# A transformer block in one kernel: the gated layer's second projection in seven products for three of its four blocks, its last bias spread over half units, four copies on ScalarE

## The chip, the core and the metric

The kernel runs on one core of one Trainium2 chip. The metric is the device time of one execution in microseconds, as the median of several executions. All arithmetic is in 32-bit floats.

## What is computed

Two batch rows of 1024 tokens with 256 features go through self-attention (16 heads of 64), cross-attention to 154 context rows, and a gated feed-forward layer, each with a layer norm ahead of it and a residual behind it. What matters here is the last layer:

```python
h = _layernorm(x, ln3_g, ln3_b)
p = h @ ff_w1 + ff_b1                      # 256 -> 2 x 1024
a, gate = (p[..., :D_FF], p[..., D_FF:])
h = a * jax.nn.gelu(gate, approximate=False) @ ff_w2 + ff_b2   # 1024 -> 256
return h + x
```

## The kernel before

The program is laid out by hand: the order in which it is written is the order in which each engine gets its instructions, and semaphores are added where one engine's result or buffer is needed by another. Three stages follow each other: self-attention, cross-attention, and the gated layer, a loop over `k` from 0 to 63. All of the change but one switch lies in that last loop; the switch is in a function that both of the last two stages call.

**Blocks, units, half units.** The 2048 tokens are four blocks ("pairs", `pair` 0 to 3) of 512 tokens, each again two halves of 256 (`BT`). The 1024 inner features are eight groups of 128 (`NF`). A unit `n` is one block and one group, `k` counts half units: even `k` runs `gate_first(k // 2)`, odd `k` runs `gate_second(k // 2)`. The first projection (`product`, L1039) already takes seven products for eight: for a unit TensorE runs products 1, 6 and 5 in the first half unit, 2, 7 and 3 in the second, and 4 (`gate_last`) in the next unit's first half, after that unit's product 1. Product 4 goes onto product 7's PSUM tile `pb` and so waits for VectorE's read of it (L1078). Each product is one call of 128x128 weights against 256 columns. ScalarE copies the first sum (L1058) and does the two Gelus (L1076, L1082); VectorE adds (L1062, L1064, L1078, L1081, L1090); GpSimd multiplies value and gate into `ub[pair]` (L1083 for the second half of the block's tokens, L1092 for the first).

**The second projection** (`sum_slot`, L1105). When the last group of a block is done, 32 slots are put in the list `sums`: four row tiles of 128 tokens, eight inner groups each, one call of 256 columns per slot. Two slots are taken in each half unit, so block 0's run in half units 16 to 31, block 1's in 32 to 47, block 2's in 48 to 63, and block 3's after the loop. After the eighth slot of a row tile VectorE adds the sum to the rows in `xt` (L1115) and a DMA sends them out, on SP's queue, or on ScalarE's for every second tile of the last block.

**Work beside it.** `side` is a list of steps of layer norms: from half unit 7 on the second batch row's norm runs, one step in each odd half unit (statistics on VectorE; deviation and normalized rows `xn` on GpSimd, L246, L250, L267; four transposes on TensorE into `ph`, L280; scaling on ScalarE). `later` is a list of small steps, one of which is taken in each half unit; in this loop they are the 16 additions of the last bias to the rows of `xt` on GpSimd (L320), eight for each batch row, put there when that row's norm is through. `token_sums` puts four GpSimd additions in half units 8, 24 and 40, for the first projection of the next block.

**Cross-attention's last two units** are finished inside the loop: `cross_values` multiplies into four PSUM tiles `poc` and copies each with VectorE (L930); part 0 uses two tiles of one PSUM pool, part 1 two of the pool `mm` from which the products' tiles `pa` come as well.

Of the kernel before, what the change touches and what calls it, by code (L numbers as in the profile page):

```python
# [18 lines left out]
def tile_transformer_block(ctx: ExitStack, tc: tile.TileContext, a: dict, out: bass.AP):  # L19
    nc = tc.nc  # L20
    x, cond = a["x"], a["ctx_768"]
# [10 lines left out]
    NT = S // P  # L32
    GT = 4
    NG = NT // GT
# [5 lines left out]
    KB = 32  # L40
# [22 lines left out]
    pt_ = ctx.enter_context(tc.tile_pool(name="pt", bufs=2))  # L63
# [33 lines left out]
    row_of, r = {}, 0  # L97
    for n in names:
        k = n_of[n]
# [458 lines left out]
    later = []  # L558
# [11 lines left out]
    def run_work(n, n_side, bank=None, n_sum=0):  # L570

        while n > 0 and work:
            n -= work[0].banks
            run(work.pop(0))
        for _ in range(min(n_side, len(side))):
            needs_bank, needs, fn = side[0]
            if needs_bank and not bank and n <= 0 or not added.issuperset(needs):  # L580
                break
            if needs_bank and not bank:
                n -= 1
            spare["bank"] = bank or mm_tile
# [316 lines left out]
    def cross_values(ui, a2):  # L901

        b, pr = units[ui]
        v, v0 = vs["ca", b, pr // 2], pr % 2 * P
        if a2 == 0 and pr % HP == 0:
            oT["ca", b, pr // HP] = pt_.tile([P, HP, S], F32, tag="oT", name=f"o_ca{b}_{pr}")
        quarters = (a2, 2 + a2)  # L910
        po = {a4: (mm_tile if a2 else sum_tile)(f"poc_{ui}_{a4}") for a4 in quarters}
        for m in range(NM + 1):
            for a4 in quarters:
                r0 = a4 // 2 * QG
                r = slice(r0, r0 + QG)
                for j in range(2):
                    nc.tensor.matmul(  # L917
                        po[a4][j * DH:(j + 1) * DH, :NT * KB],
                        lhsT=v[r, m + a2 * (m == NM), v0 + j * DH:v0 + (j + 1) * DH],
                        rhs=pTc["pairs"][r, a2, m, j] if m < NM else  # L920
                        pTc["ring"][r, ui % 3, NB - 1, j, :],
                        start=(m == 0), stop=(m == NM),
                        tile_position=(r0, j * DH),
                    )
        dst = oT["ca", b, pr // HP][:, pr % HP, :].rearrange(
            "p (t a q) -> p t a q", a=P // KB, q=KB)

        def store():
            for a4 in quarters:
                nc.vector.tensor_copy(  # L930
                    dst[:, :, a4, :], po[a4][:, :NT * KB].rearrange("p (t q) -> p t q", q=KB)
                )

        return store

# [26 lines left out]
    NPR = B * 2  # L962
    BT = S // 4
    FU = NPR * NF
    wsum, wh, ub, psum, pools = {}, {}, {}, {}, {}

    def hold_gated():

        wf = pt_.tile([P, 2 * NK, QH // 2], F32, tag="pT", name="wf").rearrange("p a b -> p (a b)")
        n1, n2 = NC * 2 * DF, NF * D  # L970
        w1 = wf[:, :n1].rearrange("p (c h f) -> p c h f", c=NC, h=2)
        w2 = wf[:, n1:n1 + n2].rearrange("p (f d) -> p f d", f=NF)
        pTc["pairs"] = wf[:, n1 + n2:n1 + n2 + 2 * NM * 2 * NT * KB].rearrange(
            "p (a m j q) -> p a m j q", a=2, m=NM, j=2)
# [15 lines left out]
        parts.extend(lambda f=f: part2(f) for f in range(0, NF, 2))  # L990
        return w1, w2, parts
# [39 lines left out]
    def product(n, i, into, first):  # L1031

        pair, f = divmod(n, NF)
        own = slice(f * P, (f + 1) * P)
        lhs = {
            1: w1[:, 0, 1, own], 2: w1[:, 1, 1, own], 3: wsum[4][:, own], 4: w1[:, 1, 0, own],
            5: wsum[1][:, own], 6: wsum[2][:, own], 7: w1[:, 0, 0, own],
        }[i]
        nc.tensor.matmul(  # L1039
            into[:, :BT], lhsT=lhs, rhs=wh[pair][i], start=first, stop=True,  # L1040
            skip_group_check=True)
# [24 lines left out]
    def biases(n):  # L1066
        c = row_of["ff_b1"] + n % NF
        return cols[:, c:c + 1], cols[:, c + NF:c + NF + 1]
# [16 lines left out]
    def gate_last(n):  # L1085

        pair, f = divmod(n, NF)
        pa, pb, pc, own = psum.pop(n)
        product(n, 4, pb, False)
        nc.vector.scalar_tensor_tensor(  # L1090
            own[:, 0, :], pb[:, :BT], biases(n)[0], own[:, 0, :], op0=ALU.add, op1=ALU.add)
        nc.gpsimd.tensor_tensor(ub[pair][0][:, f, :], own[:, 0, :], own[:, 3, :], ALU.mult)  # L1092
        if f == NF - 1:
            sums.extend((pair, i, e) for i in range(2 * TF) for e in range(NF))

    sums, summed = [], {}

    def sum_slot():

        pair, i, f = sums.pop(0)  # L1100
        if f == 0:
            summed[pair] = sum_tile(f"pf{pair}_{i}")
        own = summed[pair]
        j, e = divmod(i, TF)
        nc.tensor.matmul(  # L1105
            own[:, :D], lhsT=ub[pair][j][:, f, e * P:(e + 1) * P], rhs=w2[:, f, :],
            start=(f == 0), stop=(f == NF - 1),
        )
        if f < NF - 1:
            return None  # L1110
        b, t = divmod(pair * 2 * TF + i, NT)

        def store():
            xs = xt[b, t // GT][:, t % GT, :]
            nc.vector.tensor_tensor(xs, own[:, :D], xs, ALU.add)  # L1115
            (nc.scalar if pair == NPR - 1 and i % 2 else nc.sync).dma_start(
                out=out[b, t * P:(t + 1) * P, :], in_=xs)

        return store


    with tc.manual_schedule():
# [11 lines left out]
        own = [ps_s.tile([P, 2, HB], F32, tag="s", name=f"first_{r}") for r in range(2)]  # L1134
# [49 lines left out]
        for p in range(SA):  # L1184
# [11 lines left out]
            ui, n = divmod(p, 2 * SH)  # L1196
# [5 lines left out]
            if p < 2 * SH - 1 or p % SH in (1, 2):  # L1202
# [4 lines left out]
                f = (ui - NPAIR // 2 - 1) * EC  # L1207
# [12 lines left out]
        for c in range(CA):  # L1220
# [7 lines left out]
            if c == SH + 1:  # L1228

                w1, w2, parts = hold_gated()  # L1230
# [3 lines left out]
            ui, n = divmod(c, len(CG))  # L1234
# [75 lines left out]
        for k in range(2 * FU):  # L1310
            c = CA + k
            if k == 0:
                run_work(0, 0, n_sum=2)
            flush(adds)
            (gate_second if k % 2 else gate_first)(k // 2)
            flush(stores)
            flush(lates)
            if k == 2 * len(CG) + 1:
                norm_beside("ff", B - 1)
            if k == 0:  # L1320
                load_out("ca", B - 1, NQ - 1)
            cross_drain(c)
            if k % 2:
                cross_weigh(c - 1 if k == len(CG) + 2 else c)
            cross_regroup(c)
            if k == len(CG) + 2:
                out_pieces("ca", B - 1, NQ - 1, out_order("ca"))
            if k % (2 * NF) == NF and k < 2 * FU - 2 * NF:
                token_sums(k // (2 * NF) + 1)
            for _ in range(min(2, len(sums))):  # L1330
                run(sum_slot)
            flush(stores)
            run_work(0 if k == 1 else 1 + k % 2, k % 2)
            if later:
                later.pop(0)()
        gate_last(FU - 1)
        while sums:
            run(sum_slot)
            flush(stores)
# [33 lines left out]
```

## Time and profile before

| | |
|---|---|
| median of 3 runs | 1095.6 us (1094.71 to 1096.67) |
| the profiled execution | 1093.61 us, span 1091.8 us |
| granted TensorE clock | 0.998 |
| TensorE matmuls, busy | 1070.7 us, 98% of the span |
| GpSimd, busy | 729.9 us, 67% |
| first call of the second projection | 960.9 us from the span's start |
| its last call | 1088.2 us |

Times in the profile count from the span's start. A 32-bit matmul call shows as two records of the matmul (PE) and two of its weight load (PEld), so "x2" after a matmul is one call. A record's length contains its way through the array, so consecutive records overlap, and the distance from one start to the next tells what a record costs. In a timeline the bracket behind a line is the time that the engine was idle before it, and what ended that. The span is a little shorter than the execution's time, which has start and end around it.

### The profile page before, as it was taken

What the parts mean: (1) busy time and instruction counts of PE and PEld (TensorE: products, weight loads), DVE (VectorE), ACT (ScalarE), POOL (GpSimd) and SP (SyncE); (2) the same over time, 40 slices, a digit from 0 to 9 for tenths busy, and PEclk for the clock granted to TensorE, in tenths of its full rate; (3) what the DMA queues carried; (4) which work ended last, traced back from release to release, by engine and by line L of the source; (5) the groups of instructions that cost most, each with busy time, mean ns of one, the idle gap of its engine ahead of it and who ended that gap; (6) DMA issues with size and microseconds to landing.
All of it is one profiled execution on the core that took longest, in us unless ns stands there. A gap on an engine that the chain in (4) does not pass through costs nothing.

```text
span 1091.8 us, 44847 instructions
## 1 busy us (share of the span) xinstructions
PE 1070.7 (98%) x18388; PEld 703.4 (64%) x18388; DVE 881.2 (81%) x1301; ACT 643.5 (59%) x2057; POOL 729.9 (67%) x1552
## 2 busy tenths in 40 slices
PE   8999999999999999999999999989999999899998
PEld 6446556556566565566565665566767677788887
DVE  5799899998988989999989989868877877645442
ACT  5666766777667666667776775566555554232221
POOL 2677777877777777777777777667664785565321
PEclk9999999999999999999999999999999999999999
DMA  3222112112111111111111211136755555000000
GB/s 94 64 60 67 43 38 52 33 33 57 40 43 39 42 44 29 42 43 34 42 42 30 46 33 29 32 85 159 187 133 127 127 117 133 1 10 15 11 15 30
DMA packets 106142, 62.81 MB, mean 58 GB/s; under 512 B 32330, under 2 KB 96722, under 8 KB 105938
## 3 DMA queue, kind: packets, MB, share of 16 engines
q1 hardware_dynamic: 104562, 59.16, 22.7%
q8 instruction: 145, 2.38, 0.9%
q10 hardware_dynamic: 1376, 0.79, 0.2%
q14 instruction: 59, 0.48, 0.1%
HBM read 30.01 MB, written 2.10 MB: 29 GB/s over the span
## 4 chain that ended last, share of the span: by engine, by line
PE 89%; DVE 3%; POOL 3%; ACT 2%; DMA 2%; SPq 1%; issue 1%; ACTq 0%; DVEq 0%; POOLq 0%
PE s L493 19%; PE po L547 19%; PE py_sa L467 5%; PE pf L1105 5%; PE py_ca L467 5%; PE pv_sa L393 5%; PE pq_sa L362 5%; PE pk_sa L362 4%; PE poc L917 4%; PE pq_ca L362 4%; PE pb L1039 3%; PE sc L838 3%; PE pa L1039 2%; PE pc L1039 2%; PE ph_ln L280 1%; ACT p L508 1%
## 5 line engine op out<-in xcount | busy, mean ns | idle before, releaser
L613 POOL TENSOR_SCALAR p<-p,rd,ee 128x512 f32<-128x512 f32 x512 | 390.3, 773 | 98.1 <-DVE rd L605 93.7
L508 ACT ACTIVATE p<-s,st 128x512 f32<-128x512 f32 x512 | 345.8, 687 | 177.9 <-DVE st L502 168.9
L502 DVE TENSOR_REDUCE st<-s 128x2 f32<-128x1024 f32 x256 | 308.8, 1207 | 53.4 <-issue 16.8
L626 DVE STREAM_TRANSPOSE pT<-p 128x1024 f32<-128x1024 f32 x256 | 302.6, 1220 | 4.0 <-POOL p L613 4.0
L493 PE MATMUL s<-k_sa,q_sa 64*32 64x512 f32 x4096 | 252.0, 594 | 4.9 <-ACT p L508 4.2
L547 PE MATMUL po<-pT,v_sa 64*32 64x256 f32 x8192 | 235.8, 376 | 2.3 <-DVE pT L626 2.3
L547 PEld LDWEIGHTS po<-pT,v_sa 64*32 64x32 f32 x8192 | 169.2, 106 | 80.6 <-issue 27.1
L493 PEld LDWEIGHTS s<-k_sa,q_sa 64*32 64x32 f32 x4096 | 79.5, 106 | 106.6 <-issue 51.2
L854 ACT ACTIVATE p<-sc,neg 128x154 f32<-128x154 f32 x256 | 96.5, 407 | 83.3 <-DVE rden L862 77.2
L865 POOL TENSOR_SCALAR p<-p,rden 128x154 f32<-128x154 f32 x256 | 97.3, 401 | 60.0 <-DVE rden L862 59.6
L508 ACT ACTIVATION_READ_ACCUMULATOR p<-s,st 128x1 f32 x512 | 103.4, 202 | 0.0
L526 POOL TENSOR_TENSOR dd<-st 128x8 f32<-128x8 f32 x128 | 25.8, 202 | 68.7 <-DMA st<-st 65.5
L393 PEld LDWEIGHTS pv_sa<-sa_wv,hT_ln 64*128 64x128 f32 x1024 | 58.6, 188 | 14.2 <-issue 10.1
L393 PE MATMUL pv_sa<-sa_wv,hT_ln 64*128 64x128 f32 x1024 | 61.8, 275 | 0.0
L467 PE MATMUL py_ca<-ca_wo,o_ca 128*128 128x256 f32 x256 | 60.0, 382 | 0.5 <-DVE o_ca L930 0.5
L467 PE MATMUL py_sa<-sa_wo,o_sa 128*128 128x256 f32 x256 | 59.7, 386 | 0.0
L467 PEld LDWEIGHTS py_sa<-sa_wo,o_sa 128*128 128x128 f32 x256 | 47.3, 190 | 17.8 <-issue 6.2
L843 DVE TENSOR_REDUCE neg<-sc 128x6 f32<-128x924 f32 (+1 forms) x48 | 48.0, 1000 | 13.2 <-PE sc L838 13.1
L362 PE MATMUL pq_ca<-hT_ln,ca_wq 64*128 64x512 f32 (+1 forms) x304 | 58.2, 589 | 0.0
L854 ACT ACTIVATION_READ_ACCUMULATOR p<-sc,neg 128x1 f32 x256 | 57.1, 223 | 0.0
L362 PE MATMUL pq_sa<-hT_ln,sa_wq 64*32 64x512 f32 (+1 forms) x976 | 56.6, 586 | 0.0
L362 PE MATMUL pk_sa<-hT_ln,sa_wk 64*32 64x512 f32 x960 | 55.5, 590 | 0.0
(117 smaller groups left out, 1418.3 us busy)
## 6 DMA issues: line engine op xcount, KB each, us to landing
wf<-pT_ca SPq DMA_DIRECT2D x128, 128.0 KB, 2.4
st<-st SPq DMA_DIRECT2D x512, 1.0 KB, 1.8
v_sa<-v_sa SPq DMA_DIRECT2D x32, 256.0 KB, 4.1
sa_wq<-in_L_xattn_sa_wq_dram SPq DMA_DIRECT2D x32, 128.0 KB, 3.0
sa_wk<-in_L_xattn_sa_wk_dram SPq DMA_DIRECT2D x32, 128.0 KB, 2.9
sa_wv<-in_L_xattn_sa_wv_dram SPq DMA_DIRECT2D x32, 128.0 KB, 3.2
ca_wq<-in_L_xattn_ca_wq_dram SPq DMA_DIRECT2D x32, 128.0 KB, 3.7
wf<-in_L_xattn_ff_w_dram SPq DMA_DIRECT2D x12, 256.0 KB, 3.3
```

What stands on the lines that cost most here:

```text
L362: nc.tensor.matmul(pq[r][f:f + m, at:at + n], lhsT=wt[own, c, f:f + m], rhs=h[own, c, t0:t0 + n], start=(c == 0), stop=(c == NH - 1), tile ...
L393: nc.tensor.matmul(pv[r][:, i * P:(i + 1) * P], lhsT=h[own, c, i * P:(i + 1) * P], rhs=wt[own, c, :], start=(c == 0), stop=(c == NH - 1), ...
L467: nc.tensor.matmul(py[:, e * D:(e + 1) * D], lhsT=o[:, i, (t + e) * P:(t + e + 1) * P], rhs=wo[kind, b, g][:, i, :], start=(i == 0), stop= ...
L493: nc.tensor.matmul(sc[a4 * KB:(a4 + 1) * KB, j, :], lhsT=q[r, c:c + KB], rhs=k[r, h * HB:(h + 1) * HB], start=True, stop=True, tile_positi ...
L502: nc.vector.tensor_reduce(st[:, 0, 0, i, :], sc, AX.X, ALU.max, negate=True)
L508: nc.scalar.activation(pr[:, j, :], sc[:, j, :], AF.Exp, bias=st[:, 0, 0, i, j:j + 1], accum_out=st[:, 0, 1, i, j:j + 1],)
L547: nc.tensor.matmul(po[a2][d:d + KB, :QH // 2], lhsT=v[r, t, e, d:d + KB], rhs=pT[r, d // DH * NK + n, :], start=(t == 0 and e == 0), stop= ...
L613: nc.gpsimd.tensor_scalar(pr[:, j, :], pr[:, j, :], v["rd"][:, c:c + 1], v["ee"][:, 0, c:c + 1], op0=ALU.mult, op1=ALU.mult,)
L626: nc.vector.transpose(halves[h][:, :, c:c + KB], slot[p]["members"][i].rearrange("p j (n k) -> p (j n) k", k=KB))
L854: nc.scalar.activation(pr_[:, j, i, :T], sc[:, j, i * T:(i + 1) * T], AF.Exp, bias=neg[:, j, i:i + 1], accum_out=den[:, j, i:i + 1],)
L865: nc.gpsimd.tensor_scalar(pr_[:, j, i, :T], pr_[:, j, i, :T], rden[:, j, i:i + 1], 1.0, op0=ALU.mult, op1=ALU.mult,)
L1039: nc.tensor.matmul(into[:, :BT], lhsT=lhs, rhs=wh[pair][i], start=first, stop=True, skip_group_check=True)
```

## The change

Four things are changed.

1. In `cross_values`, when the gated layer's PSUM pool is open, one of the two copies of each part goes to ScalarE. This holds for the two units that are finished inside the loop, four copies in all.
2. The steps in `later` are taken only when `k > 12` and `k % 3 == 1`, so the 16 bias additions fall in half units 13, 16, 19 and so on to 58.
3. For blocks 1 to 3 the second projection takes seven products for eight. The block's tokens and the inner groups (even and odd) form a two by two matrix of `ub`; the inner groups and the output's two halves of 128 columns form one of the weights. Four sums of weights (`column_sums`, 128x512 each) are made once, in half units 18, 20, 24 and 26; four sums of `ub` (`row_sums`, 128x256 each) are made for each pair of inner groups, four times a block, from half unit 21 on, all on GpSimd, the last four after the loop. They lie in the buffer that held cross-attention's transposed weights. A slot is then one product for one of two row tiles: four calls of 128x128 weights against 128 columns. There are 14 slots a block; block 0 keeps its 32 slots of before, two in a half unit, and from half unit 32 on there is one slot in a half unit. A row tile's sums go into two PSUM tiles, `into` (products 2, 3, 4, 5, in four column ranges) and `own` (product 1 in the first 128 columns, product 6 in the next, and product 7 added onto product 6 after VectorE has read that).
4. The sums of the seven products are formed by the residual additions on VectorE: after product 1 to all four quarters (128x512), after 6 to one (128x128), after 3 from `into` to all four (128x512) and from its last range once more to one (128x128), after 7 to two (128x256). Rows of the first half go out after product 3, of the second after 7. The last block's slots run in the order 1, 4, 2 for both row tiles, then 5, 6, 3, 7 for one and for the other.

```diff
+        shared = pools.get("f") is not None
         def store():
             for a4 in quarters:
-                nc.vector.tensor_copy(
-                    dst[:, :, a4, :], po[a4][:, :NT * KB].rearrange("p (t q) -> p t q", q=KB)
-                )
+                own = po[a4][:, :NT * KB].rearrange("p (t q) -> p t q", q=KB)
+                if shared and a4 == a2:
+                    nc.scalar.copy(dst[:, :, a4, :], own)
+                else:
+                    nc.vector.tensor_copy(dst[:, :, a4, :], own)
...
         if f == NF - 1:
-            sums.extend((pair, i, e) for i in range(2 * TF) for e in range(NF))
+            if pair:
+                early, late = (1, 4, 2), (5, 6, 3, 7)
+                if pair == NPR - 1:
+                    sums.extend((pair, i, m) for m in early for i in range(TF))
+                    sums.extend((pair, i, m) for i in range(TF) for m in late)
+                else:
+                    sums.extend((pair, i, m) for i in range(TF) for m in early + late)
+            else:
+                sums.extend((pair, i, e) for i in range(2 * TF) for e in range(NF))
...
+    def column_sums(n):
+        t = half["t"]
+        nc.gpsimd.tensor_tensor(*[
+            lambda: (t[5], quarter(0, 1), quarter(0, 0)),
+            lambda: (t[6], quarter(1, 1), t[5]),
+            lambda: (t[4], quarter(1, 0), t[6]),
+            lambda: (t[7], quarter(1, 1), quarter(0, 1)),
+        ][n](), ALU.subtract)
+
+    def row_sums(pair, c):
+        s = {i: own[:, c, :] for i, own in half["s"][pair % 2].items()}
+        (a11, a12), (a21, a22) = ([ub[pair][j][:, 2 * c + e, :] for e in range(2)] for j in range(2))
+        tt = nc.gpsimd.tensor_tensor
+        tt(s[5], a21, a22, ALU.add)
+        tt(s[6], s[5], a11, ALU.subtract)
+        tt(s[3], a12, s[6], ALU.subtract)
+        tt(a21, a11, a21, ALU.subtract)
+
+    def partial(pair, i, m):
+        if m == 1:
+            bank = mm_tile if pair == NPR - 1 and i else sum_tile
+            summed[pair, i] = [bank(f"pf{pair}_{i}_{r}") for r in range(2)]
+        into, own = summed[pair, i]
+        at = {2: 0, 3: 1, 4: 2, 5: 3}.get(m)
+        region = own[:, (m != 1) * P:][:, :P] if at is None else into[:, at * P:(at + 1) * P]
...
+        for c in range(NF // 2):
...
+            nc.tensor.matmul(
+                region, lhsT=lhs, rhs=rhs, start=(c == 0 and m != 7), stop=(c == NF // 2 - 1),
+                skip_group_check=True)
+        if m in (2, 4, 5):
+            return None
...
+        def store():
+            if m == 1:
+                plus(xs, region.unsqueeze(1).unsqueeze(1).broadcast_to([P, 2, 2, P]))
+            elif m == 6:
+                plus(xs[:, 0, 1], region)
+            elif m == 3:
+                plus(xs, into.rearrange("p (j d k) -> p j d k", j=2, d=2))
+                plus(xs[:, 0, 1], into[:, 3 * P:4 * P])
+                send(0, nc.sync)
+            else:
+                plus(xs[:, 1], region.unsqueeze(1).broadcast_to([P, 2, P]))
+                send(1, nc.scalar if pair == NPR - 1 and i else nc.sync)
...
-            (nc.scalar if pair == NPR - 1 and i % 2 else nc.sync).dma_start(
-                out=out[b, t * P:(t + 1) * P, :], in_=xs)
+            nc.sync.dma_start(out=out[b, t * P:(t + 1) * P, :], in_=xs)
...
-            for _ in range(min(2, len(sums))):
+            for _ in range(min(2 if k < 4 * NF else 1, len(sums))):
                 run(sum_slot)
             flush(stores)
             run_work(0 if k == 1 else 1 + k % 2, k % 2)
-            if later:
+            if later and k > 12 and k % 3 == 1:
                 later.pop(0)()
+            if k == 2 * NF:
+                hold_sums()
+            if k in (2 * NF + 2, 2 * NF + 4, 2 * NF + 8, 2 * NF + 10):
+                column_sums((k - 2 * NF) // 3)
+            pair, at = divmod(k - 5, 2 * NF)
+            if pair > 0 and at % 4 == 0:
+                row_sums(pair, at // 4)
         gate_last(FU - 1)
+        row_sums(NPR - 1, NF // 2 - 1)
         while sums:
             run(sum_slot)
             flush(stores)
```

More of the change, by code (lines that the diff above doesn't have):

```diff
@@ new lines, in tile_transformer_block, with hold_sums @@
+    sums, summed = [], {}
+    half = {}
+    def hold_sums():
+        wx = pt_.tile([P, 2 * NK, QH // 2], F32, tag="pT", name="wx").rearrange("p a b -> p (a b)")
+        n1, n2 = NF // 2 * P, NF // 2 * BT
+        half["t"] = {
+            i: wx[:, k * n1:(k + 1) * n1].rearrange("p (c d) -> p c d", d=P)
+            for k, i in enumerate((5, 6, 7, 4))
+        }
+        half["s"] = [
+            {
+                i: wx[:, 4 * n1 + (3 * e + k) * n2:][:, :n2].rearrange("p (c t) -> p c t", t=BT)
+                for k, i in enumerate((5, 6, 3))
+            }
+            for e in range(2)
+        ]
@@ new lines, in quarter @@
+    def quarter(odd, d):
+        return w2[:, odd::2, d * P:(d + 1) * P]
+    def column_sums(n):
[14 more added lines that the diff above has]
+        tt(a21, a11, a21, ALU.subtract)
@@ new lines, in partial, with plus, send @@
+    def partial(pair, i, m):
[5 more added lines that the diff above has]
+        region = own[:, (m != 1) * P:][:, :P] if at is None else into[:, at * P:(at + 1) * P]
+        token = slice(i * P, (i + 1) * P)
+        for c in range(NF // 2):
+            lhs = {
+                1: lambda: ub[pair][0][:, 2 * c, token], 2: lambda: ub[pair][0][:, 2 * c + 1, token],
+                4: lambda: ub[pair][1][:, 2 * c + 1, token], 7: lambda: ub[pair][1][:, 2 * c, token],
+            }.get(m, lambda: half["s"][pair % 2][m][:, c, token])()
+            rhs = {1: (0, 0), 2: (1, 0), 3: (1, 1)}.get(m)
+            rhs = half["t"][m][:, c, :] if rhs is None else quarter(*rhs)[:, c, :]
+            nc.tensor.matmul(
[3 more added lines that the diff above has]
+            return None
+        b, g = divmod(pair, NG)
+        xs = xt[b, g].rearrange("p (j i) (d k) -> p i j d k", i=TF, k=P)[:, i]
+        def plus(x, y):
+            nc.vector.tensor_tensor(x, y, x, ALU.add)
+        def send(j, queue):
+            t = 2 * TF * pair % NT + j * TF + i
+            queue.dma_start(out=out[b, t * P:(t + 1) * P, :], in_=xt[b, g][:, j * TF + i, :])
+        def store():
[10 more added lines that the diff above has]
+                send(1, nc.scalar if pair == NPR - 1 and i else nc.sync)
+        return store
@@ L1098, in sum_slot @@
     def sum_slot():
         pair, i, f = sums.pop(0)
+        if pair:
+            return partial(pair, i, f)
         if f == 0:
```

## The prediction

> **What bounds the kernel now.** I read the first two blocks of the page, then the busy time by stretches of the gated layer, then the timeline of TensorE and of GpSimd there.
>
> ```profile
> PE 1070.7 (98%) x18388; PEld 703.4 (64%) x18388; DVE 881.2 (81%) x1301; ACT 643.5 (59%) x2057; POOL 729.9 (67%) x1552
> ...
> PE   8999999999999999999999999989999999899998
> ...
> 945.00:950.00 5.00, 4.86 (x23) 3.78 (x22) 4.40 (x16) 2.01 (x5) 4.84 (x9) 1.00 0.00 0
> 950.00:955.00 5.00, 2.61 (x13) 1.62 (x12) 2.98 (x10) 0.98 (x2) 4.84 (x9) 1.00 0.00 0
> 955.00:960.00 5.00, 4.02 (x20) 3.03 (x19) 2.38 (x6) 2.28 (x5) 4.84 (x9) 1.00 0.01 3
> 960.00:965.00 5.00, 5.00 (x27) 4.39 (x26) 2.19 (x6) 2.28 (x5) 3.47 (x7) 1.00 0.00 0
> ```
>
> TensorE bounds the whole: 98% of the span. The columns of the stretches are PE, PEld, DVE, ACT, POOL, then the granted clock (1.00 throughout). Only the stretch 945 to 960 has TensorE idle, and there GpSimd is full (4.84 of each 5 us). From 960 until the end of the matmuls TensorE is busy in every stretch. So two things can shorten the layer: less GpSimd work ahead of TensorE before 960, and less TensorE time after it. The change does both, and touches nothing ahead of the layer: its copy switch needs the PSUM pool that opens with it.
>
> **The bias adds.** Before, one bias add is issued on GpSimd in each half unit as soon as there is one; after, none before half unit 13, then one in three. No DMA moves with them.
>
> ```profile
> 946.24 0.59 PE L1039 MATMUL pa<-hT_ln,wf 128*128 128x256 f32 x2
> 946.97 0.70 PE L1039 MATMUL pb<-hT_ln,wf 128*128 128x256 f32 x2
> ...
> 949.66 0.59 PE L1039 MATMUL pa<-hT_ln,wf 128*128 128x256 f32 x2
> 950.63 0.70 PE L1039 MATMUL pb<-hT_ln,wf 128*128 128x256 f32 x2 [0.38 <-DVE own L1062]
> 951.17 0.59 PE L1039 MATMUL pc<-hT_ln,w1s 128*128 128x256 f32 x2
> 953.56 0.33 PE L280 MATMUL ph_ln<-ident,xn_ln 128*128 128x128 f32 x1 [1.79 <-POOL xn_ln L267]
> 954.10 0.55 PE L280 MATMUL ph_ln<-ident,xn_ln 128*128 128x128 f32 x3 [0.21 <-POOL xn_ln L267]
> 954.49 0.60 PE L1039 MATMUL pa<-hT_ln,wf 128*128 128x256 f32 x2
> ...
> 958.44 0.33 PE L280 MATMUL ph_ln<-ident,xn_ln 128*128 128x128 f32 x1 [0.77 <-POOL xn_ln L267]
> ...
> 959.37 0.60 PE L1039 MATMUL pa<-hT_ln,wf 128*128 128x256 f32 x2
> ```
>
> A matmul call is two records here. From 946.24 to 959.37 TensorE issues 17 calls and two groups of four transposes. A call takes 0.432 us where nothing stalls (two records at the 0.216 worked out below), a group as much: 19 x 0.432 = 8.2 us. It took 13.1, so 4.9 us are lost. Of these 0.30 and 0.54 are the two late pb (946.97 and 950.63, where 946.67 and 950.09 were due), which wait for VectorE; the rest waits for the normalized rows xn, which stand in GpSimd's queue behind bias adds:
>
> ```profile
> 946.67 0.73 POOL L320 TENSOR_TENSOR x<-x,ff_b 128x256 f32<-128x256 f32 x1
> ...
> 949.11 0.73 POOL L320 TENSOR_TENSOR x<-x,ff_b 128x256 f32<-128x256 f32 x1
> ...
> 950.48 0.72 POOL L320 TENSOR_TENSOR x<-x,ff_b 128x256 f32<-128x256 f32 x1
> 951.17 0.72 POOL L1083 TENSOR_TENSOR kT<-own 128x256 f32<-128x256 f32 x1
> ...
> 952.95 1.10 POOL L267 TENSOR_SCALAR xn_ln<-x,rstd_ln,off_ln 128x256 f32<-128x256 f32 x2
> 954.01 0.72 POOL L320 TENSOR_TENSOR x<-x,ff_b 128x256 f32<-128x256 f32 x1
> ...
> 955.37 0.73 POOL L320 TENSOR_TENSOR x<-x,ff_b 128x256 f32<-128x256 f32 x1
> ...
> 957.83 1.10 POOL L267 TENSOR_SCALAR xn_ln<-x,rstd_ln,off_ln 128x256 f32<-128x256 f32 x2
> ```
>
> An add holds the queue for 0.69 us (950.48 to 951.17). Three go from ahead of the first xn, so it starts at 952.95 - 2.07 = 950.88 and its second half is there at 951.98. TensorE arrives at 951.17 + 0.43 = 951.60, so it loses about 0.4 instead of 2.5 (954.49 less 951.60 less 0.43). The second xn has five adds fewer ahead of it: 957.83 - 3.45 = 954.38, done at 955.48; TensorE, after four transposes and seven calls, is there at about 955.4. What is late next is VectorE, with the same 0.84. Gain 4.9 - 0.84 - 0.4 = **3.7 us**. Bounds: 4.9 if VectorE's lateness goes too, 2.5 if the queue drains 1.2 us worse than this shift, as it may where an operand becomes the later one. The adds return from half unit 13 on, always ahead of the residual add of their rows, into a stage where TensorE waits for nobody.
>
> **The second projection.** Before, each block of 512 tokens took 32 calls of 256 columns; after, three blocks take 7 products x 2 row tiles x 4 = 56 calls of 128 columns, each with its own 128x128 weight load. Inside the loop a slot goes from two long calls to four short ones, and 14 half units carry one where 16 did.
>
> ```profile
> 1074.42 13.79 PEld L1105 LDWEIGHTS pf<-wf,u 128*128 128x128 f32 x64
> ...
> 1074.64 13.98 PE L1105 MATMUL pf<-wf,u 128*128 128x256 f32 x64
> ...
> 46.39 3.84 PE L393 MATMUL pv_sa<-sa_wv,hT_ln 64*128 64x128 f32 x64
> 50.16 1.95 PE L493 MATMUL s<-k_sa,q_sa 64*32 64x512 f32 x32
> ...
> 964.12 0.60 PE L280 MATMUL ph_ln<-ident,xn_ln 128*128 128x128 f32 x4
> 964.55 0.60 PE L1039 MATMUL pa<-hT_ln,wf 128*128 128x256 f32 x2
> ...
> L1105 PEld LDWEIGHTS pf<-wf,u 128*128 128x128 f32 x224 | 42.6, 190 | 5.8
> L1105 PE MATMUL pf<-wf,u 128*128 128x256 f32 x224 | 55.0, 379 | 0.0
> ...
> L280 PEld LDWEIGHTS ph_ln<-ident,xn_ln 128*128 128x128 f32 x16 | 1.9, 140 | 4.4 <-POOL xn_ln L267 4.2
> ...
> L393 PE MATMUL pv_sa<-sa_wv,hT_ln 64*128 64x128 f32 x1024 | 61.8, 275 | 0.0
> ```
>
> The last block, 64 records, takes 13.98 us; less the tail of one record (0.379) over 63 that is 0.216 us a record, 13.8 us a block. A load is recorded with 0.190 us, yet the pair keeps to 0.216: the loads run under the matmuls. For 128 columns under a full 128x128 load of this kind the trace has no row, so I bound it. From below: four full-array transposes of 128 columns follow each other in 0.43 us, 0.1075 a record, though with a shorter load (0.140). From above: the values' projection, 128 columns under 128-column loads in two row groups side by side, runs 64 records from 46.39 to 50.16, two at a time: 0.118. The same row without its own tail, (3.84 - 0.275)/63 x 2, gives 0.113, and I take that, because its load has the same columns. A block is then 112 x 0.113 = 12.7 us, 1.17 less; three blocks **3.5 us** (5.3 with 0.1075, 1.9 with 0.118).
>
> The Trainium skill's page "TensorE: Matmul & The Clock Gate", section "Back-to-back issue gap", speaks against this. It says that in a stream of load and matmul pairs the spacing is set by both, about 81 ns at 128 columns where the matmul alone needs 56. By that ratio (an estimate from that page) a record of 0.108, half of 0.216, would take 0.156, a block 17.5 us, and the kernel would come to about 1103 us. The pv row, a stream of just such pairs, has 0.113 and is nearer.
>
> **What the seven products need elsewhere.**
>
> ```profile
> L1092 POOL TENSOR_TENSOR u<-own 128x256 f32<-128x256 f32 x29 | 21.1, 729 | 10.5 <-DVE own L1090 10.4
> L1115 DVE TENSOR_TENSOR x<-pf,x 128x256 f32<-128x256 f32 x16 | 6.8, 425 | 17.3 <-PE pf L1105 17.3
> L474 DVE TENSOR_TENSOR x<-py_ca,x 128x512 f32<-128x512 f32 x1 | 0.7, 693 | 0.2 <-PE py_ca L467 0.2
> ```
>
> GpSimd gets 48 row sums like L1092's operation (0.7 us apart, 34 us) and four column sums of twice the width (below 1.4 each, 5.6). Half units 16 to 31 are fullest. TensorE needs 16 x 2.37 = 38 us there (3.5 calls and a slot of two each, 5.5 x 0.432), plus 0.9 of transposes; GpSimd needs 16 products (11), the column sums (5.6), three row-sum groups (8.4), six biases (4.2), one token sum (2.8) and two xn pairs with their deviation (3): 35. It fits, but in half units 24 and 25 about 9 us meet 4.7, so the queue is some 4 us late. Who waits: the next products only, whose buffers have several units of slack, until half unit 35, where product 5 needs the row sum issued at the end of 33; in 27 to 32 8.4 us of work meet 14 us, so by then the queue is empty. Cost nothing; if the cover is gone, up to 4 us once.
>
> VectorE's residual adds grow from 2 x 0.425 to about 2.4 us per row tile (two 128x512 at 0.693, one 128x256, two 128x128 at about 0.29, an estimate by the slope between 256 and 512 columns). VectorE is busy 2.19 of 5 us in the last stretch quoted first, so this hides. Product 7 adds onto product 6 in PSUM and waits for VectorE's read of it; product 3, eight records or 0.9 us, stands between, against a drain of 0.27, 0.29 for the add and the signals. No stall, at most 0.2 us in six places.
>
> In the last two half units no slot is left, and the last pb call follows its pc at once:
>
> ```profile
> 1072.91 0.59 PE L1039 MATMUL pc<-hT_ln,w1s 128*128 128x256 f32 x2
> 1073.11 0.48 DVE L1078 SCALAR_TENSOR_TENSOR own<-pb,cols,own 128x256 f32<-128x256 f32 x1 [1.30 <-PE pb L1039]
> ...
> 1074.21 0.59 PE L1039 MATMUL pb<-hs,wf 128*128 128x256 f32 x2
> ```
>
> It may start only after VectorE's read, at 1073.59 instead of 1073.34, plus a cold load: **0.4 us lost**. In the final block the row sums are queued for about 4.5 us from its start, and product 5 comes after 5.4 us of products 1, 4 and 2: hidden. The output DMAs stay 16; one more goes to SP, and the last is ACT's as before.
>
> **The ScalarE copies** (four of 128x256, two at each of two cross-attention units): the matmul after them waits for the first copy's bank, which either engine frees equally late. Nothing, between 0.4 gained and 0.4 lost.
>
> **Sum:** -3.7 - 3.5 + 0.4 = -6.8 us. The profiled execution took 1093.6 (span 1091.8), 2.0 below the median 1095.6; it would come to 1086.8, the median to **1088.8 us**.
>
> **The rivals.**
> Short calls gain nothing: at 0.1235 a record (13.8/112) a block takes what it took, and only the bias part is left: -3.3, 1092.3. For it: overheads at 56 short calls; against: the pv row.
> Bias adds gain nothing because VectorE and the operands of xn are late anyway: -3.1, 1092.5. Against: GpSimd's queue has no gap there.
> GpSimd becomes the bound around half units 24 to 35, 4 us lost: -2.8, 1092.8. For it: 35 of 39 us; against: buffers and the empty half units before 33.
> The other side, one mechanism: weight loads of 128 columns no longer fit under 128-column matmuls in the full array, where no second row group helps, so each record waits for part of its load. If the recorded 0.190 is the period, a block takes 21.3 us, 7.5 more: -3.3 + 22.4 = +19, 1114.7. Half of the way there from 0.118, 0.154, a block takes 17.2, 3.4 more: +7.0, **1102.6**, the price I give it. It decides from 0.133 a record on, where the three blocks eat the other gains. For it: load and matmul are equally long for the first time; against: the transposes, full array, at 0.1075. The Trainium skill's rule named above is this rival, and would put it at about 1103.
>
> **How the numbers follow.** The forecast has 0.62, with a range of its own from 1085.5 (4.9 + 5.3) to 1091.5 (2.5 + 1.9); short calls without gain 0.13, bias without gain 0.06, GpSimd 0.09, weight loads 0.10 (0.07 of it near 0.154). About 0.2% (2.2 us) is what a measurement of this kernel tells from no change, so the line lies at 1093.4. The three weak cases lie just below it, and a third of them would be called no change: faster 0.81, same 0.09, slower 0.10. The range takes them in: 1085.5 to 1093.3.
>
> **What would show it.** Right: TensorE above 4.7 of 5 us between 945 and 960, waits for xn below 1 us together, pf records of 128 columns 0.108 to 0.118 apart, the final 112 records in 12 to 13.2 us, and no TensorE wait for GpSimd after half unit 20. Wrong: pf records 0.13 or more apart, or waits for wx or u in half units 24 to 38.

## The result and the profile after

The changed kernel takes 1090.46 us (median of 5 runs, 1087.98 to 1092.78), the kernel before beside it 1095.73 (5 runs, 1094.71 to 1096.67): a ratio of 0.9951, interval 0.9937 to 0.9966, 5.3 us less. The profiled execution took 1092.04 us, its span is 1090.2.

The page's first two blocks, engine by engine:

```profile
PE 1069.7 (98%) x18532; PEld 704.8 (65%) x18532; DVE 888.9 (82%) x1315; ACT 644.9 (59%) x2061; POOL 767.7 (70%) x1604
...
PE   8999999999999999999999999989999999999998
```

TensorE still bounds the kernel. GpSimd's busy time grew by 38 us (729.9 to 767.7), where the prediction counted 34 + 5.6 for the new additions. In the stretches of the layer (columns as in the prediction):

```profile
950.00:955.00 5.00, 4.72 (x21) 3.44 (x19) 4.40 (x16) 1.88 (x6) 4.66 (x9) 1.00 0.00 0
955.00:960.00 5.00, 4.53 (x22) 3.65 (x23) 4.03 (x13) 2.65 (x6) 4.68 (x9) 1.00 0.00 0
...
980.00:990.00 10.00, 10.00 (x48) 8.79 (x48) 5.13 (x13) 2.73 (x7) 9.61 (x14) 1.00 0.05 15
990.00:1000.00 10.00, 10.00 (x48) 8.81 (x47) 4.72 (x12) 3.20 (x7) 9.61 (x14) 1.00 0.04 14
```

The hole in TensorE's time is nearly closed: the worst stretch has 4.53 of 5 us where before one had 2.61 (above 4.7 was predicted for all of 945 to 960, which holds but for this one; 960 to 965 has 4.96). The last two rows are the fullest on GpSimd, 96%, and TensorE has no gap there.

What TensorE waited for from 905 us on (us in total, times, the longest), first before and then after:

```profile
PE ph_ln L280 <- POOL xn_ln L267: 3.0, 4, 1.8
...
PE pb L1039 <- DVE own L1062: 0.4, 1, 0.4
```

```profile
PE pb L1043 <- DVE own L1066: 0.5, 1, 0.5
...
PE ph_ln L280 <- POOL xn_ln L267: 0.2, 1, 0.2
```

The wait for the normalized rows is down from 3.0 us to 0.2. The wait for VectorE (L1062 of before is L1066 of after) stayed, 0.4 before and 0.5 now.

**Where the time went.** The stages ahead of the layer are the same in both kernels, yet the layer starts 4.7 us later in this profile of after (its first product, the first pa call, starts at 916.68, in the profile of before at 911.97). So I compare stretches of the layer, each from the start of one call to the start of another:

| stretch | before | after | difference |
|---|---|---|---|
| first pa call to the pa of half unit 16 | 47.40 | 44.14 | -3.26 |
| half unit 16 to 32 (block 0, unchanged slots) | 38.86 | 38.86 | 0 |
| half unit 32 to 48 (block 1) | 37.99 | 36.68 | -1.31 |
| half unit 48 to the last pb (block 2) | 37.99 | 36.99 | -1.00 |
| the last pb to the end of the matmuls (block 3) | 14.41 | 13.60 | -0.81 |
| the layer | 176.65 | 170.27 | -6.38 |

The layer lost 6.4 us where the prediction had 6.8. The same layer took 170.2 in a second profile of the changed kernel. The median moved by 5.3 only. The difference lies outside the layer, whose start scatters: in nine profiles, of all kernels here, the first pa came between 911.1 and 916.7 us.

TensorE's timeline around the first slots in seven products, and at the end:

```profile
1001.41 1.05 PE L1167 MATMUL pf<-wf,u 128*128 128x128 f32 x8
1002.30 0.60 PE L1043 MATMUL pa<-hT_ln,wf 128*128 128x256 f32 x2
...
1072.61 0.59 PE L1043 MATMUL pc<-hT_ln,w1s 128*128 128x256 f32 x2
1073.35 0.70 PE L1043 MATMUL pb<-hs,wf 128*128 128x256 f32 x2
1073.89 2.34 PE L1167 MATMUL pf<-wf,u 128*128 128x128 f32 x16
1076.06 1.95 PE L1167 MATMUL pf<-wx,u 128*128 128x128 f32 x16
...
1085.89 1.06 PE L1167 MATMUL pf<-wx,u 128*128 128x128 f32 x8
```

A slot of eight records takes 1.05 us less its share of overlap: the next call starts 0.89 after it, 0.111 us a record. The last pb is 0.31 late (due at 1073.04) and the call behind it follows after 0.54 and not 0.43, which was expected; the first 16 records of block 3 take 2.17 us to the next start where the later ones take 1.79, which was not. The weight loads show who was late there:

```profile
1074.84 1.19 PEld L1167 LDWEIGHTS pf<-wf,u 128*128 128x128 f32 x10 [0.32 <-POOL u L1096]
```

and GpSimd's timeline shows why:

```profile
1071.08 0.73 POOL L1146 TENSOR_TENSOR wx<-u 128x256 f32<-128x256 f32 x1
...
1073.37 0.73 POOL L1149 TENSOR_TENSOR u<-u,u 128x256 f32<-128x256 f32 x1
1074.05 0.74 POOL L1096 TENSOR_TENSOR u<-own 128x256 f32<-128x256 f32 x1
```

Product 1 of the last block needs the value that L1096 writes for unit 30. It stands behind the four row sums issued in half unit 61, 3 us of work, and so ends at 1074.79; the load follows 0.05 later. That is a wait the prediction did not have: no wait for GpSimd after half unit 20 was one of its signs of being right, and this sign failed.

### The profile page after: what moved, and what is told of

Same layout as the page of the kernel before. It is cut to its first block, busy times and chain, and to the rows that moved or that the text cites. A ratio compares the mean times of both kernels' runs of the same rounds, so it can differ in the third digit from the quotient of the medians.

```text
span 1090.2 us, 45214 instructions
## 1 busy us (share of the span) xinstructions
PE 1069.7 (98%) x18532; PEld 704.8 (65%) x18532; DVE 888.9 (82%) x1315; ACT 644.9 (59%) x2061; POOL 767.7 (70%) x1604
## 4 chain that ended last, share of the span: by engine, by line
PE 89%; DVE 3%; POOL 2%; ACT 2%; DMA 2%; SPq 1%; issue 1%; DVEq 0%; ACTq 0%; POOLq 0%
PE po L547 20%; PE s L493 19%; PE py_sa L467 5%; PE pv_sa L393 5%; PE py_ca L467 5%; PE pq_sa L362 5%; PE pk_sa L362 5%; PE poc L917 4%; PE pq_ca L362 3%; PE pb L1043 3%; PE pf L1167 3%; PE sc L838 3%; PE pa L1043 2%; PE pc L1043 2%; PE pf L1206 1%; PE ph_ln L280 1%
## 5 line engine op out<-in xcount | busy, mean ns | idle before, releaser
L547 PE MATMUL po<-pT,v_sa 64*32 64x256 f32 x8192 | 240.0, 379 | 2.3 <-DVE pT L626 2.3
```

Source lines behind the costliest of these rows:

```text
L547: nc.tensor.matmul(po[a2][d:d + KB, :QH // 2], lhsT=v[r, t, e, d:d + KB], rhs=pT[r, d // DH * NK + n, :], start=(t == 0 and e == 0), stop= ...
```

## The experiments

All of them compute the whole output; the edits are against the kernel named.

**1. The bias rule alone** (against the kernel before). It tells the bias term from the rest.

```diff
-            if later:
+            if later and k > 12 and k % 3 == 1:
```

> The kernel before with one edit: the bias additions only after half unit 12 and in every third half unit. Theory (the 4.9 us lost ahead of half unit 16 were bias additions ahead of xn in GpSimd's queue): from the layer's first pa call to its first pf call 3 to 3.5 us less than before, from there on the same within 0.2 us; whole run 3 us faster, within the scatter of the unchanged stages ahead. Rival (VectorE and the operands of xn are late anyway): under 1 us less in that stretch.

Measured: 1090.56 us (10 runs) against 1094.05 (29 runs), ratio 0.9965, interval 0.9953 to 0.9977 (ratios are to the kernel before, here and below). From the first pa to the first call of the second projection (its matmul, in before at 961.09; the 960.9 of the table of before is the start of its weight load) it took 45.95 us where before took 49.12, so 3.2 less; from there to the end 127.53, as before. The term is real, it lies where it was put, and it needs nothing from the other parts.

**2. The seven products alone** (against the kernel after).

```diff
-        shared = pools.get("f") is not None
+        shared = False
...
-            if later and k > 12 and k % 3 == 1:
+            if later:
```

> The changed kernel with the bias additions one in each half unit as before and all copies on VectorE; only the seven products are left of the change. Theory (each of the three blocks gains by itself: 112 records at 0.111 us): from the layer's first pa to its first pf call as before, 42.3 us for the 16 half units with 14 slots less by 1.3 us in each of blocks 1 and 2, the part after the loop shorter by 0.8, whole layer 3.1 us shorter than before. Rival (the two parts need each other, since GpSimd has row sums, column sums and bias additions together): TensorE waits for GpSimd between half units 16 and 40, and less than 2 us are gained.

Measured: 1092.74 us (10 runs), ratio 0.9987, interval 0.9975 to 0.9999. To the first call of the second projection 49.09 us, as before (the granted clock fell to 0.83 between 950 and 960 us, where TensorE waits for xn, and the stretch is no longer for it); from there 125.41, 2.1 less and not 3.1. The missing microsecond went to one place, TensorE's first slot in seven products (half unit 32), which takes 1.92 to the next call (1003.05) and not 0.89:

```profile
1001.13 0.83 PE L1167 MATMUL pf<-wf,u 128*128 128x128 f32 x6
1002.72 0.49 PE L1167 MATMUL pf<-wf,u 128*128 128x128 f32 x2 [0.76 <-POOL u L1096]
```

with GpSimd at the same time:

```profile
996.22 0.73 POOL L320 TENSOR_TENSOR x<-x,ff_b 128x256 f32<-128x256 f32 x1
...
1001.94 0.73 POOL L1096 TENSOR_TENSOR u<-own 128x256 f32<-128x256 f32 x1
```

The slot's last call was due at 1001.80 (six records of 0.111); it needs the value of 1001.94 and gets it at 1002.67. With a bias addition in each half unit, eight of them stand in GpSimd's queue between 976 and 999 us, where the changed kernel has three, and its value (999.12, shown in experiment 6) starts 3.1 us earlier, both counted from half unit 32's pa. So the bias rule is worth 3.2 us by itself and another 1.0 as cover for the seven products.

**3. The ScalarE copies alone** (against the kernel before; the diff is that of the front, with the same condition).

> The kernel before with only the four copies on ScalarE. Theory: nothing, since the call behind them waits for the first copy's bank, which ScalarE frees 0.05 us earlier; layer within 0.2 us of before. Rival: two copies side by side free the bank 0.38 us earlier at each of two places, 0.8 us less.

Measured: 1094.3 us (10 runs), ratio 0.9996, interval 0.9983 to 1.0009; the layer took 176.5, before 176.65. The waits of TensorE:

```profile
PE py_ca L467 <- ACT o_ca L932: 0.5, 1, 0.5
PE pa L1041 <- ACT o_ca L932: 0.5, 1, 0.5
```

Before they were two waits of 0.5 for VectorE's copies; now they are two of 0.5 for ScalarE's. The releaser has another name and the wait is the same.

**4. The changed kernel once more**, beside 1 to 3.

> The changed kernel once more. Theory (the layer is 6.3 us shorter, and the unchanged stages ahead of it vary by some 4 us from execution to execution, whatever the kernel): the layer's first pa call falls anywhere between 911 and 918 us, the layer takes 170.3 us within 0.3, and the ratio's interval holds 0.9943 (6.3 us). Rival (the change slows the stages ahead of the layer, by 4.7 us in the profiled execution): the first pa call again at 916 to 917, while the kernels that leave the seven products out have it near 912.

Measured: 1088.13 us (6 runs), ratio 0.994, interval 0.9922 to 0.9958. The layer took 170.2 us, and started at 915.47: within the theory's range and half a microsecond below the rival's, so this run alone does not part the two. What the starts of all nine profiles show stands at the end of the next section.

**5. Each call of 128 columns split in two of 64**, each with its own load (against the kernel after). If a load needs longer than its 64 columns of matmul, the distance between records is the load's period.

```diff
-            nc.tensor.matmul(
-                region, lhsT=lhs, rhs=rhs, start=(c == 0 and m != 7), stop=(c == NF // 2 - 1),
+            for r0 in range(0, P, P // 2):
+                cols64 = slice(r0, r0 + P // 2)
+                nc.tensor.matmul(
+                    region[:, cols64], lhsT=lhs, rhs=rhs[:, cols64],
+                    start=(c == 0 and m != 7 and r0 == 0), stop=(c == NF // 2 - 1),
```

> The changed kernel with every 128-column call of the seven products split into two calls of 64 columns, each with its own weight load. It asks how near the load is to setting the pace. Theory (a 128-column load needs about 0.107 us, as long as the matmul of 128 columns, and is hidden only just): records of 64 columns stay 0.107 to 0.115 us apart, a slot of 16 records takes 1.8 us instead of 0.89, and the 42 slots make the layer 37 us longer. Rival (loads have room to spare, the pace is the matmul's and would follow the columns): 0.06 us apart, slots of 0.95 us, the layer within 3 us. Rival (the recorded 0.190 us is the period where a load has nothing to hide under): 3 us a slot, 90 us longer.

Measured: 1124.87 us in a single execution (the kernel before, beside it, 1096.37), layer 207.3, 37.1 longer than after's. TensorE's timeline in the last block:

```profile
1101.81 3.74 PE L1169 MATMUL pf<-wf,u 128*128 128x64 f32 x32
1105.39 3.74 PE L1169 MATMUL pf<-wx 128*128 128x64 f32 x32
```

and the loads of one kind, grouped from 1000 us on (records, busy time, mean of one):

```profile
L1169 PEld LDWEIGHTS pf<-wx 128*128 128x128 f32 x192 | 22.9, 192 | 0.4
```

32 records from 1101.81 to 1105.39 are 0.112 us each. The matmul's part, a quarter of the 0.216 of 256 columns, would be 0.054 (an estimate). So something else sets the pace, and 0.112 is what the 128-column records keep too, 0.111. The nearest cause is the load: its period is then 0.112, although each load is recorded with 0.192. A fixed cost of every record would give the same distances, but the starts speak against it. Where a slot follows a call of 256 columns, its first load had that call to run under (it starts 0.214 us ahead of its matmul, later loads 0.055), and the slot's second record starts 0.055 us after its first (997.231 and 997.287); from the third on the distance is 0.111 to 0.112, as it is between the loads. In the changed kernel the first two records of such slots are 0.109 apart. So at 128 columns matmul (0.109) and load (0.112) are equal within 3%, and the load is the longer. At 64 columns nothing more was gained. No run changes the load alone, so that it is the load is read from these distances and not tested by itself.

**6. A bias addition in each half unit from 13 on**, not in each third (against the kernel after). All 16 additions then come ahead of block 1's first slot.

```diff
-            if later and k > 12 and k % 3 == 1:
+            if later and k > 12:
```

> The changed kernel with one bias addition in every half unit from 13 on instead of every third. Nine more of them, 0.69 us each, then stand ahead of half unit 32 in GpSimd's queue, which before had the last operand of block 1's first slot ready 2.2 us ahead of TensorE. Theory (the cover is those 2.2 us): TensorE waits about 6.2 - 2.2 = 4 us for u in half unit 32, and the layer takes 174 us instead of 170.3. Rival (the buffers ahead take it up, GpSimd's lateness costs nothing): no wait over 0.5 us, 170.3 us.

Measured: 1088.88 us (4 runs) against 1096.37 (11 runs), ratio 0.9935, interval 0.9913 to 0.9957; layer 171.2, not the 174 expected. TensorE's timeline in half unit 32:

```profile
996.18 0.83 PE L1167 MATMUL pf<-wf,u 128*128 128x128 f32 x6
997.76 0.49 PE L1167 MATMUL pf<-wf,u 128*128 128x128 f32 x2 [0.75 <-POOL u L1096]
```

The wait is where it was expected, but only 1.0 us is lost by it (1.91 to the next call at 998.09, not 0.89). My expectation set the further additions against the 2.2 us by which the value is early in the changed kernel, and forgot GpSimd's idle gaps, which this timeline of GpSimd in the changed kernel shows:

```profile
968.41 1.27 POOL L1134 TENSOR_TENSOR wx<-wf 128x512 f32<-128x512 f32 x1
971.14 0.73 POOL L1087 TENSOR_TENSOR u<-own 128x256 f32<-128x256 f32 x1 [1.46 <-ACT own L1086]
...
976.33 0.72 POOL L1087 TENSOR_TENSOR u<-own 128x256 f32<-128x256 f32 x1 [1.55 <-ACT own L1086]
...
999.12 0.73 POOL L1096 TENSOR_TENSOR u<-own 128x256 f32<-128x256 f32 x1
...
1001.44 0.73 POOL L1096 TENSOR_TENSOR u<-own 128x256 f32<-128x256 f32 x1
1004.84 0.73 POOL L1087 TENSOR_TENSOR u<-own 128x256 f32<-128x256 f32 x1 [2.68 <-ACT own L1086]
```

The value of 999.12 is there at 999.85, and TensorE takes it at about 1002.08 (1001.41 and six records of 0.111): 2.2 us early. Ahead of it lie 1.46 and 1.55 us of idle time, with two smaller gaps (0.27 and 0.23) 3.5, and they fill first. Cover is the lead and the gaps together, 5.7 us. Sixteen additions instead of six ahead of the value are ten times 0.69, 6.9 us: 1.2 too many. Counted from half unit 32's pa, the value came 3.1 us later than in the changed kernel, 0.9 after it was due. The last row is for later: GpSimd goes idle at 1002.17, for 2.68 us, so its queue is empty in half unit 32. And the stretch to the first call of the second projection is 45.85 us here, 45.86 in the changed kernel: the 3.2 us come from holding the additions back until half unit 13, not from taking every third half unit afterwards.

**7. The end in another order** (against the kernel after): row sums one half unit later, behind L1096, and the last pb behind the last block's first slot.

```diff
-            pair, at = divmod(k - 5, 2 * NF)
+            pair, at = divmod(k - 6, 2 * NF)
...
+        run(lambda: partial(NPR - 1, 0, 1))
         gate_last(FU - 1)
         row_sums(NPR - 1, NF // 2 - 1)
+        sums.pop(0)
```

> The changed kernel with two steps moved: each group of row sums one half unit later, behind the product that it held up, and the last block's first slot ahead of the last pb call. Theory (0.39 us behind u and 0.31 us behind VectorE's read of pb are lost at the loop's end): both go, the layer takes 169.6 us instead of 170.3, and TensorE has no wait after half unit 14; a whole run 0.7 us less, which the scatter hides. Rival (the row sums, moved, come too late for product 5 in half units 35 and 51): a new wait there of up to 2 us.

Measured: 1088.07 us (6 runs) against 1096.37, ratio 0.9926, interval 0.9908 to 0.9943; layer 169.7, 0.6 less than after's. TensorE's timeline:

```profile
1070.06 0.59 PE L1043 MATMUL pc<-hT_ln,w1s 128*128 128x256 f32 x2
1070.49 1.05 PE L1167 MATMUL pf<-wf,u 128*128 128x128 f32 x8
1071.38 0.60 PE L1043 MATMUL pb<-hs,wf 128*128 128x256 f32 x2
1071.81 1.05 PE L1167 MATMUL pf<-wf,u 128*128 128x128 f32 x8
1072.70 2.21 PE L1167 MATMUL pf<-wx,u 128*128 128x128 f32 x16
1074.75 1.95 PE L1167 MATMUL pf<-wf,u 128*128 128x128 f32 x16
```

Both late places of after are gone: pb follows at once, and product 1 runs in 0.89 a slot. About 0.26 us turned up in the slot at 1072.70 (2.05 to the next start, not 1.79): GpSimd has L1087 of unit 31, which writes the last operand of product 4, behind the same row sums (1072.75 to 1073.48). This order has the shortest layer of all versions. That the whole kernel is faster than the changed one is not shown: 0.6 us lies below the scatter of the stages ahead.

## Why the prediction was right, and where not

The direction, the two places and their sizes came out as predicted: 1090.5 in the range, against 1088.8. The forecast was 1.7 us too low; 0.4 of it is the layer (6.4 gained for 6.8), and the rest lies outside it, where the kernels have the same instructions and the layer's start scatters. That the layer's sum is so near is in part luck: each of its three terms was off by 0.4, the bias adds and the end for the worse and the seven products for the better.

**Bias adds: predicted 3.7, measured 3.2 to 3.3.** The shift of GpSimd's queue came as worked out. GpSimd's and TensorE's timelines of after are 4.66 us behind those of before (pa of half unit 2: 924.37 and 919.71):

```profile
955.56 1.10 POOL L267 TENSOR_SCALAR xn_ln<-x,rstd_ln,off_ln 128x256 f32<-128x256 f32 x2
...
959.28 1.10 POOL L267 TENSOR_SCALAR xn_ln<-x,rstd_ln,off_ln 128x256 f32<-128x256 f32 x2
```

```profile
950.84 0.59 PE L1043 MATMUL pa<-hT_ln,wf 128*128 128x256 f32 x2
951.58 0.70 PE L1043 MATMUL pb<-hT_ln,wf 128*128 128x256 f32 x2
952.11 0.59 PE L1043 MATMUL pc<-hT_ln,w1s 128*128 128x256 f32 x2
...
954.27 0.59 PE L1043 MATMUL pa<-hT_ln,wf 128*128 128x256 f32 x2
955.31 0.70 PE L1043 MATMUL pb<-hT_ln,wf 128*128 128x256 f32 x2 [0.45 <-DVE own L1066]
955.85 0.59 PE L1043 MATMUL pc<-hT_ln,w1s 128*128 128x256 f32 x2
956.28 0.27 PE L280 MATMUL ph_ln<-ident,xn_ln 128*128 128x128 f32 x1
956.72 0.55 PE L280 MATMUL ph_ln<-ident,xn_ln 128*128 128x128 f32 x3 [0.16 <-POOL xn_ln L267]
957.10 0.60 PE L1043 MATMUL pa<-hT_ln,wf 128*128 128x256 f32 x2
...
960.12 0.86 PE L280 MATMUL ph_ln<-ident,xn_ln 128*128 128x128 f32 x4
960.82 0.60 PE L1043 MATMUL pa<-hT_ln,wf 128*128 128x256 f32 x2
```

The first xn starts at 955.56 - 4.66 = 950.90, predicted 950.88; TensorE arrives at 956.28 - 4.66 = 951.62, predicted 951.60, and loses 0.39 (0.82 for a group of 0.43), predicted 0.4. The second xn starts at 954.62, predicted 954.38, so its second half comes 0.24 later, and its group takes 0.70: 0.27 more, where nothing was foreseen. The rest of the error is the remainder "from VectorE": the two late pb are 0.31 and 0.61 late, and the call behind each follows after 0.53 and 0.54 and not 0.43, which is 0.21 more. I had counted that restart in the 4.9 that is lost before, and not in the 0.84 that stays. What stays is thus 1.13 + 0.66 = 1.8 instead of 1.24; 4.9 less 1.8 is 3.1, within 0.2 of the measured.

**Seven products: predicted 3.5, measured 3.9** without the waits (1.31 in block 1, in block 2 the 1.00 of the table and the last pb's 0.31, and in block 3 the 0.81 of the table, 0.38 for the late value and 0.11 for the call behind the late pb). The record took 0.111 where 0.113 was taken and 0.1075 to 0.118 were the bounds. The value was right. The reason beside it, that loads run under the matmuls, holds at 256 columns; at 128 it is the other way round by a hair, since by experiment 5 the load is the longer. The pv row has the same columns in the load, which was the reason for taking it, and so it gave nearly the load's period; the prediction did not know that this is what it took.

The rule of the Trainium skill's page "TensorE: Matmul & The Clock Gate", section "Back-to-back issue gap", would by its ratio have made a record 0.156 us (an estimate); the trace does not agree, 0.111. The same page's section "LDWEIGHTS (loading the stationary operand)" gives a load's time as its columns over 1.2 GHz, 107 ns for 128 columns, whatever the rows: experiment 5 agrees within 5%, 0.112, when it is taken as the period of each record, two a call.

**Short calls, bias adds and weight loads as rivals** fall by these numbers, and by experiments 1 and 2, which test the two parts one at a time. The last had a true core: each record does wait for its load, but for 0.002 to 0.003 us (0.111 to 0.112 for 0.109), not for the 0.02 or more that would have eaten the gains.

**GpSimd's cover: cost nothing in the loop**, as predicted (no wait in half units 16 to 60, queue empty after 1002.17). But it was nearer than "several units of slack" in half unit 32: 2.2 us. Experiments 2 and 6 crossed that edge and lost 1.0 us each; the rival's 4 us, which put all the queue's lateness on TensorE, was not seen.

**The end: predicted 0.4, measured 0.8.** The late pb cost 0.31, and 0.11 behind it, as predicted. The claim that block 3's row sums are hidden was wrong at one place: I looked at who needs the row sums (product 5, hidden), and not at which operand of the very first product stands behind them in the queue. That cost 0.38. Experiment 7 removed both, and lost 0.26 in another place.

**VectorE's additions** took 0.291 for 128x128, estimated at 0.29:

```profile
L1176 DVE TENSOR_TENSOR x<-pf,x 128x512 f32<-128x512 f32 x12 | 8.3, 692 | 6.2 <-PE pf L1167 6.2
...
L1176 DVE TENSOR_TENSOR x<-pf,x 128x128 f32<-128x128 f32 x12 | 3.5, 291 | 8.0 <-PE pf L1167 7.8
```

Most of their idle time ends with TensorE, so they wait for it and not it for them. Product 7 behind product 6's read did not stall: in block 3 the starts from 1076.06 to 1085.89 are 88 records apart, 0.112 each, with no hole.

**The copies: nothing, as predicted**, by experiment 3. The prediction's sentence that only 945 to 960 has TensorE idle is not exact: before also has 4.49 of 5 us in 915 to 920 and in 930 to 935, the two waits of 0.5 for the copies.

**The start of the layer** scatters by 5 us, and in part this is TensorE's granted clock. Of the 4.7 us between the profiles of before and after, 2.0 arise between the last score matmul of self-attention and the first pa, that is in cross-attention: 215.6 us in before, 217.6 in after. Between 720 and 730 us the granted clock was 0.83 in after and 1.00 in before. The profiles of experiments 4 and 7 have the same dip, and took 217.6 and 218.0 us there; the six profiles without it took 215.2 to 215.8. In each of the three it begins about 1 us after a gap of 2.2 us in TensorE's work; all nine profiles have that gap, and why only three have the dip is not shown. Lower clocks come in the kernel before too: of its 29 executions beside experiments 1 to 4, the five with a mean clock of 0.994 or 0.995 took 1096.3 to 1098.0 us, the sixteen with 0.998 or more 1092.9 to 1095.3.

The other 2.7 us are there by the last score matmul of self-attention, and their cause stays open. It came between 696.2 and 699.1 us in the six profiles with the seven products, and between 695.8 and 696.4 in the three without. No edit changes an instruction of the stages ahead, and experiment 6, which has all parts, is among the early ones (696.3); but nine profiles don't exclude that the larger program costs something there.

## What to carry to other kernels

Where one engine's queue carries work with a due time and work without one, hold the latter back around the due times: here that gave 3.2 us with no arithmetic saved, and it made room for what another part moved to that engine. Before moving work onto a queue, ask not only who needs the new results but which old ones now stand behind it, at the first use above all; the cover there is the lead of that value plus the idle gaps ahead of it. Trading long matmuls for shorter ones pays down to the width where the matmul equals its weight load's period (here 128 columns), which is read from the distance between records and not from their length.

## What the hardware showed that was not expected

- A 128-column weight load is recorded with 0.190 to 0.192 us and follows the one before after 0.112 (experiment 5): most of the recorded length overlaps. Matmuls of 64 and of 128 columns came at the same distance, 0.112 and 0.111 us.
- A stall costs more than the bracket in a timeline says: in experiments 2 and 6 brackets of 0.76 and 0.75 us stood for 1.0 lost each. The idle time is counted from the end of the record before, whose tail would have overlapped (0.16 of it), and the next call came 0.11 later than in a running stream; after each late pb it came 0.10 to 0.11 later too.
- Executions of one kernel differ by several us (before: 1092.9 to 1098.0 in 29 executions), and in the profiles the difference lies in stages that no edit touched: the first pa lay between 911.1 and 916.7 us in nine profiles of all kernels, while the layer of the changed kernel repeated within 0.1 (170.27 and 170.2).
- One dip of the granted clock to 0.83 over 10 us, near 720 us, went with a cross-attention stage longer by about 2 us, in three profiles of nine.
